# A recommender kernel on one core: all table rows fetched by GpSimd's indirect DMAs, in place of a split over five engines

## The chip, the cores and the metric

The kernel runs on one core of a Trainium2 chip. A core has five engines that matter here: TensorE (PE in the profile, with its weight loads as PEld), VectorE (DVE), ScalarE (ACT), GpSimd (POOL) and SyncE (SP). Each takes its own list of instructions in order and waits on semaphores that other engines, or landing DMAs, raise. The metric is the device time of one execution in microseconds; three runs of the kernel before took 49978.42, 49955.76 and 49929.08 us, median 49955.76.

## The reference

There are 50001 items. Every item has two embeddings of 32 numbers (`E_in`, `E_out`) and 32 neighbours. First, for each item and each of the two tables, the item attends to its neighbours:

```python
def _neighbor_attn(E, near_full):
    V = E[near_full]                       # 50001 x 32 neighbours x 32
    scores = jnp.einsum('nd,nkd->nk', E, V) / jnp.sqrt(jnp.float32(GEO_HALF))
    w = jax.nn.softmax(scores, axis=-1)
    return jnp.einsum('nk,nkd->nd', w, V)

a_sus = _neighbor_attn(E_in, near_full)
a_inf = _neighbor_attn(E_out, near_full)
h = jnp.concatenate([E_hist[history], a_sus[history], a_inf[history]], axis=-1)
t = jnp.concatenate([E_tgt[target], a_inf[target], a_sus[target]], axis=-1)
x = h * t[:, None, :]                      # 16384 users x 100 x 128
z = jax.nn.relu(jnp.einsum('bld,hd->blh', x, W1) + b1)
scores = jnp.einsum('blh,h->bl', z, W2[0])
```

Then each of 16384 users has a history of 100 items and one target item. The rows of the history are multiplied with the target's row, go through a small two-layer network, and the exponentials of the scores, masked and normalised, weight the history's rows. The total over all users and all features, one number, then enters a cosine with each target's row, and a sigmoid gives the 16384 outputs. All of it is float32.

## The kernel before

The two embeddings of an item lie side by side in `egeo`, one row of 64 numbers (256 bytes) for each item, padded to 23 x 17 x 128 = 50048 rows. The kernel has two stages.

**Stage 1** builds two tables of 128 numbers per item in DRAM, `table` (for histories) and `ttab` (for targets). It works on 391 subtiles `s` of 128 items, 17 to an iteration. An iteration's neighbour numbers `nidx` come with one DMA (`load`). For a subtile, tile `v` holds 32 neighbours' rows for each of 128 items. One indirect DMA of GpSimd (line 256) fetches one neighbour for all 128 items: 128 rows of 256 bytes, at addresses that it takes from a column of `nidx`. Tile `v` has three buffers (`n_v`, `bufs=3`). Then VectorE multiplies `v` with the item's own row (`products`, line 336), sums to scores (`scores`, 346), takes the largest (`largest`, 354 and 355); ScalarE makes the exponentials (`exponents`, 363); VectorE weights `v` (`weighted`, 377, twice), sums (`attend`, 388 and 390) and divides (`attended`, 402). A software pipeline spreads this over the steps `s`, `s+1`, `s+2` and `s+3`. Its second `weighted` is the last reader of a buffer of `v`; gathers for subtile `s+3` wait for it. The order of PE, ACT, DVE and SP in stage 1 is the program's (`manual_schedule`).

From the seventh subtile on (`NFIRST = 6`), GpSimd does not fetch all 32 neighbours. The table `egeo` is also held in SBUF, transposed (two items to a column, each number as three bfloat16 parts that add up to the float32; `transposed`, lines 184 to 202). The last six neighbours are copied out of it column by column, one instruction for one row of the 128 items: by TensorE as a multiplication with an identity (line 273), or by ScalarE or VectorE as a 6-byte copy (line 277). Each takes its address from a register; `registers` (line 204) loads 16 or 32 of these at a time. `AUX` and `COLUMN` say which engine takes which neighbour. `turn` (line 300) transposes the columns back on TensorE and adds the three parts, and `even` and `odd_half` (320, 326) copy the right half of a pair into `v`. In four of seven subtiles (`BY_ROW`) one more neighbour is fetched by SP, as 128 single DMAs of one row each (line 244), with addresses from registers. So GpSimd issues 9982 gathers in stage 1, 25.5 for a subtile on average.

**Stage 2** follows an all-engine barrier (line 516). Users stand 128 to a chunk `c` (128 chunks), and a chunk's 100 history items go in 12 groups of eight and one of four. One indirect DMA of GpSimd (line 632) fetches one history item for 128 users from `table`: 128 rows of 512 bytes. Tile `h` of a group of eight has six buffers (`u_h`). TensorE transposes the eight (647), VectorE multiplies by the target (649) and sums `h` (652), TensorE and ScalarE do the first layer (667, 668), TensorE the second (676). One gather more for each chunk fetches the targets' rows (561). SP fetches two groups of eight out of every 42 such pairs (`UNIT = 42`) row by row (`one_by_one`, line 615: 2048 single DMAs), issued two units ahead, into tile `hs` with two buffers.

Of the kernel before, what the change touches and what calls it, by code (L numbers as in the profile page):

```python
# [12 lines left out]
BF16 = mybir.dt.bfloat16  # L13
# [7 lines left out]
P = 128  # L21
# [22 lines left out]
AUX = ("PPPPPPPP", "PPPPPPPP", "AAAAAAAA", "AAAAAADD", "DDDDDDDD")  # L44
NAUX = 1 + len(AUX)
COLUMN = "PDAPP"
BY_ROW = "S.S.S.S"
NFIRST = 6
ENGINE = {"A": E.Activation, "D": E.DVE, "P": E.PE}
RUN = {"A": 16, "D": 16, "P": 32}  # L50
NREG = 32
PAIRS = ROWS // 2
NST = 3
PL = 3
GROUPS = (0, 6, 12, NSUB)

# [3 lines left out]
NG = L // LG  # L62

UG = 2
UNIT = 42
AHEAD = 4
# [3 lines left out]
def kernel(  # L70
# [18 lines left out]
    ident = nc.alloc_sbuf_tensor("ident", (P, P), F32).ap()  # L89
    ones = nc.alloc_sbuf_tensor("ones", (P, P), F32).ap()  # L90
    w1T = nc.alloc_sbuf_tensor("w1T", (D, HID), F32).ap()
    ident_b = nc.alloc_sbuf_tensor("ident_b", (P, P), BF16).ap()
    small = nc.alloc_sbuf_tensor("small", (P, 8), F32).ap()
    b1_sb = small[:, 0:1]
    w2_sb = small[:, 1:2]
# [6 lines left out]

    geo_held = nc.sbuf_tensor("geo", (P, PAIRS, PL), BF16)
    geo = geo_held.__enter__().ap()
    geo_at = nc.sbuf_base - 2 * PL * PAIRS
    geo_b = geo.rearrange("d c t -> d (c t)").bitcast(U8)

    make_identity(nc, ident)
    nc.vector.tensor_copy(ident_b, ident)
    nc.vector.memset(ones, 1.0)  # L110
    nc.sync.dma_start(b1_sb, b1.rearrange("(h o) -> h o", o=1))
    nc.sync.dma_start(w2_sb, w2.rearrange("o h -> h o"))
    with (
        tc.tile_pool(name="wsb", bufs=1) as wsb,
        tc.tile_pool(name="wps", bufs=1, space=bass.MemoryType.PSUM) as wps,
    ):
        w1_sb = wsb.tile([HID, D], F32, name="w1_sb")
        nc.sync.dma_start(w1_sb, w1)
        w1_ps = wps.tile([D, HID], F32, name="w1_ps")
        nc.tensor.transpose(w1_ps, w1_sb, ident)  # L120
        nc.vector.tensor_copy(w1T, w1_ps)
# [4 lines left out]
    egeo_v = egeo.rearrange("(i p j) d -> i p j d", p=P, j=NSUB)  # L126
    table_v = table.rearrange("(i p j) d -> i p j d", p=P, j=NSUB)
    egeo_p = egeo.rearrange("(c t) d -> c (t d)", t=2)
# [4 lines left out]
    nc.scalar.dma_start(table[:, 0:DE], ehist)  # L133
    with (
        tc.manual_schedule(engines={E.PE, E.Activation, E.DVE, E.SP}),
        tc.tile_pool(name="n_st", bufs=2) as n_st,
        tc.tile_pool(name="n_in", bufs=2) as n_in,
        tc.tile_pool(name="n_v", bufs=3) as n_v,
        tc.tile_pool(name="n_p", bufs=1) as n_p,
        tc.tile_pool(name="n_g", bufs=2) as n_g,  # L140
        tc.tile_pool(name="n_s", bufs=3) as n_s,
        tc.tile_pool(name="n_ps", bufs=1, space=bass.MemoryType.PSUM) as n_ps,
        tc.tile_pool(name="n_pb", bufs=1, space=bass.MemoryType.PSUM) as n_pb,
        tc.tile_pool(name="n_pt", bufs=2, space=bass.MemoryType.PSUM) as n_pt,
        tc.tile_pool(name="n_pc", bufs=2, space=bass.MemoryType.PSUM) as n_pc,
    ):
        egeo_b = egeo.bitcast(U8).rearrange("(o r) d -> o (r d)", o=1)
        its = {}
        subs = {}
        owns = {}  # L150

        def load(it):
            nidx = n_in.tile([P, NSUB, K], I32, name="nidx")
            nc.sync.dma_start(nidx, near_v[it])

            colf = n_p.tile([P, NSUB, NAUX + 1], F32, name="colf")
            coli = n_p.tile([P, NSUB, NAUX], I32, name="coli")
            aux = nidx[:, :, K - NAUX : K]  # L160
            nc.vector.tensor_scalar(coli, aux, 1, None, ALU.logical_shift_right)
            nc.vector.tensor_copy(colf[:, :, 1 : NAUX + 1], coli)
            nc.vector.tensor_scalar(
                colf[:, :, 1 : NAUX + 1],
                colf[:, :, 1 : NAUX + 1],
                float(2 * PL),
                float(geo_at),
                ALU.mult,
                ALU.add,
            )  # L170
            nc.vector.tensor_copy(colf[:, :, 0:1], nidx[:, :, K - NAUX - 1 : K - NAUX])
            nc.vector.tensor_scalar(
                colf[:, :, 0:1], colf[:, :, 0:1], float(8 * G), None, ALU.mult
            )
            odd = n_in.tile([P, NSUB, NAUX], I32, name="odd")
            nc.vector.tensor_scalar(odd, aux, 1, None, ALU.bitwise_and)
            n = NSUB * (NAUX + 1)
            col_ps = n_pt.tile([P, NST, P], F32, name="pt")
            nc.tensor.transpose(col_ps[0:n, 0, :], colf.rearrange("p j a -> p (j a)"), ident)
            cols = n_in.tile([n, P], I32, name="cols")  # L180
            nc.vector.tensor_copy(cols, col_ps[0:n, 0, :])
            its[it] = (nidx, odd, cols)

        def transposed(q):

            h = min(P, (PAIRS - q * NST * P))
            n = NST if h == P else 1
            st = n_st.tile([P, NST, 4 * G], F32, name="st")
            base = q * NST * P
            nc.sync.dma_start(  # L190
                st[0:h, 0:n, :],
                egeo_p[base : base + h * n, :].rearrange("(p n) d -> p n d", n=n),
            )
            into = geo[:, base : base + h * n, :].rearrange("d (p n) t -> d n p t", n=n)
            ps = n_pt.tile([P, NST, P], F32, name="pt")
            for r in range(n):
                nc.tensor.transpose(ps[:, r, 0:h], st[0:h, r, :], ident[0:h, 0:h])
            rest = ps[:, 0:n, 0:h]
            for t in range(PL):
                nc.scalar.copy(into[:, :, :, t], rest)  # L200
                if t < PL - 1:
                    nc.vector.tensor_tensor(rest, rest, into[:, :, :, t], ALU.subtract)

        def registers(s, a, engine, i0, n, low, top):
            it, j = divmod(s, NSUB)
            r = j * (NAUX + 1) + a
            _, vals = nc.values_load_multi_w_load_instructions(
                its[it][2][r : r + 1, i0 : i0 + n],
                engines=[engine],
                min_val=low,  # L210
                max_val=top,
                skip_runtime_bounds_check_because="worked out from an item's number",
            )
            return vals

        def fourth(s):
            return COLUMN[s % len(COLUMN)]

        def by_row(s):
            return s >= NFIRST and BY_ROW[s % len(BY_ROW)] == "S"  # L220

        def own_rows(s):
            if s < NT:
                it, j = divmod(s, NSUB)
                owns[s] = n_s.tile([P, 2 * G], F32, name="own")
                nc.sync.dma_start(owns[s], egeo_v[it][:, j, :])

        def gather(s):
            it, j = divmod(s, NSUB)
            nidx = its[it][0]  # L230
            v = n_v.tile([P, K, 2, G], F32, name="v")
            subs[s].update(v=v)
            if s >= NFIRST:
                for a in range(NAUX):
                    if (AUX[a - 1][0] if a else fourth(s)) in "AD":
                        subs[s]["g"][a] = n_g.tile([P, P, PL], BF16, name=f"g{a}")
            own_rows(s + 1)
            if by_row(s):
                one = n_s.tile([P, 2 * G], F32, name="one")
                subs[s]["one"] = one  # L240
                for i0 in range(0, P, NREG):
                    vals = registers(s, 0, E.SP, i0, NREG, 0, (ITEMS - 1) * 8 * G)
                    for i in range(NREG):
                        nc.sync.dma_start(
                            one[i0 + i : i0 + i + 1, :].bitcast(U8),
                            egeo_b[:, ds(vals[i], 8 * G)],
                        )
            ks = list(range(K))
            if s >= NFIRST:
                ks = ks[0 : K - NAUX + 1]  # L250
                if fourth(s) != ".":
                    ks.remove(K - NAUX)
                if by_row(s):
                    ks.remove(K - NAUX - 1)
            for k in ks:
                nc.gpsimd.indirect_dma_start(  # L256
                    out=v[:, k].rearrange("p t d -> p (t d)"),
                    out_offset=None,
                    in_=egeo,
                    in_offset=bass.IndirectOffsetOnAxis(ap=nidx[:, j, k : k + 1], axis=0),  # L260
                )

        def columns(s, a, i0):

# [28 lines left out]
        def turn(s):  # L293
            if s < NFIRST:
                return
# [506 lines left out]
```

## Time and profile before

The profiled execution took 49978.42 us, with a span of 49976.7 us from its first to its last instruction. It is one of the three runs; it lies 22.7 us (0.05%) above their median.

| what | value |
|---|---|
| span; profiled execution's time | 49976.7 us; 49978.42 us |
| stage 1, first to last gather | 8.6 to 24943.3 us |
| stage 2, first to last gather | 25000.8 to 49939.5 us |
| gathers of stage 1 (line 256) | 9982 |
| gathers of stage 2 (lines 632 and 561) | 12512 + 128 |
| SP's single-row DMAs (lines 244; 615) | 28160; 36864 |
| column copies on PE; ACT; DVE | 128128; 96096; 71456 |

How to read it: a group's line gives the source line, engine, operation, tiles written and read, count, then busy time and mean length of one instruction, and the time that the engine sat idle just before such an instruction, with what ended that idle time. "issue" means that the engine waited for nothing that the profile shows. A line of the timeline gives the start and the length in us, and, in brackets, the idle time before it and what ended that.

### The profile page before, as it was taken

To read this page: it belongs to the slowest core of one execution; us is meant where nothing else is said; L and a number is where in the kernel's file an instruction comes from. 1 tells how busy PE (TensorE), PEld (TensorE's weight loads), DVE (VectorE), ACT (ScalarE), POOL (GpSimd) and SP (SyncE) were. 2 spreads that over 40 slices of the span, in tenths; PEclk is the share of its full clock that TensorE was granted. 3 is DMA by queue.
4 is the path that set the end of the run, shared out by engine and by line. 5 is a ranking of instruction groups with operands and counts; after the bars stand their busy time and mean duration, and the time that the engine had idled before them with its cause. 6 is when DMAs were issued, how large, how long until landed. Compare 5 with 4: busy or idle time off the path is not lost. (4 is left out here: it accounts for less than half of the span.)

```text
span 49976.7 us, 727656 instructions
## 1 busy us (share of the span) xinstructions
PE 16337.4 (33%) x180208; PEld 12247.4 (25%) x180208; DVE 14789.9 (30%) x80038; ACT 14133.7 (28%) x103967; POOL 21346.3 (43%) x22628
## 2 busy tenths in 40 slices
PE   1222222222222222222244444444444444444444
PEld 1111111111111111111133222322222332222222
DVE  3444444444444444444411111111111111111111
ACT  5444444444444444444400000000000000000000
POOL 3333333333333333333355444444444554444444
PEclk9999999999999999999966666666666666666666
DMA  2000000000000000000011111111111111111111
GB/s 46 17 17 17 16 16 17 17 17 17 17 17 17 17 17 17 17 16 17 16 41 36 34 34 34 34 34 34 34 33 34 38 38 35 34 34 34 34 34 33
DMA packets 1135038, 1319.89 MB, mean 26 GB/s; under 512 B 716160, under 2 KB 765888, under 8 KB 1130784
## 3 DMA queue, kind: packets, MB, share of 16 engines
q0 software_dynamic: 723904, 1156.91, 10.3%
q1 hardware_dynamic: 204288, 65.09, 0.5%
q10 hardware_dynamic: 202592, 51.31, 0.5%
q8 instruction: 1431, 23.45, 0.2%
q14 instruction: 2823, 23.13, 0.2%
HBM read 1245.88 MB, written 51.30 MB: 26 GB/s over the span
## 5 line engine op out<-in xcount | busy, mean ns | idle before, releaser
L256 POOL DMA_INDIRECT v<-in_egeo_dram,nidx x9982 | 9421.0, 944 | 15521.9 <-issue 9728.5
L632 POOL DMA_INDIRECT h<-table,hidx x12512 | 11803.9, 943 | 8706.1 <-issue 6686.9
L277 ACT COPY g<-geo 128x6 uint8 x96096 | 10608.3, 194 | 10352.0 <-issue 8540.7
L273 PE MATMUL pc<-geo,ident_b 128*128 x128128 | 4645.3, 167 | 13959.0 <-issue 12611.7
L277 DVE COPY g<-geo 128x6 uint8 x71456 | 6458.9, 175 | 7294.4 <-issue 7284.9
L668 ACT ACTIVATE z<-z_ps,small 128x512 f32<-128x512 f32 x3200 | 2187.4, 687 | 20371.5 <-PE z_ps L667 10631.0
L273 PEld LDWEIGHTS <-ident_b 128*128 128x128 bf16 x128128 | 4096.4, 105 | 14603.2 <-issue 14601.0
L649 DVE TENSOR_TENSOR xT<-hT_ps,tT 128x1024 f32<-128x1024 f32 (+1 forms) x1664 | 1967.6, 1182 | 18197.1 <-PE hT_ps L647 9437.8
L667 PE MATMUL z_ps<-xT,w1T 128*128 128x512 f32 x6400 | 5046.6, 889 | 3861.5 <-DVE xT L649 2915.8
L676 PE MATMUL score<-small,z 128*128 128x1 f32 x25600 | 4190.6, 285 | 5506.8 <-ACT z L668 3409.4
L676 PEld LDWEIGHTS score<-small,z 128*128 128x128 f32 x25600 | 4254.0, 251 | 5914.5 <-ACT z L668 3614.9
L647 PE MATMUL hT_ps<-ident,h 128*128 128x128 f32 x12512 | 3087.4, 348 | 338.3 <-issue 240.7
L647 PEld LDWEIGHTS hT_ps<-ident,h 128*128 128x128 f32 x12512 | 2360.1, 206 | 2613.2 <-issue 2363.7
L667 PEld LDWEIGHTS z_ps<-xT,w1T 128*128 128x128 f32 x6400 | 1441.8, 275 | 4473.0 <-DVE xT L649 3147.9
L300 PE MATMUL back<-ident_b,g 128*128 128x128 bf16 x6930 | 806.1, 309 | 4829.0 <-ACT g L277 2867.8
L561 POOL DMA_INDIRECT t<-ttab,tidx x128 | 120.7, 943 | 4365.4 <-ACT z L668 4275.4
L326 DVE COPY_PREDICATED v<-odd,back 128x384 f32<-128x384 int32 x385 | 225.2, 585 | 5820.5 <-ACT v L320 5819.6
L652 DVE TENSOR_REDUCE hsum<-h 128x8 f32<-128x1024 f32 (+1 forms) x1628 | 1898.5, 1166 | 0.0
L300 PEld LDWEIGHTS <-g 128*128 128x128 bf16 x6930 | 707.6, 144 | 4843.0 <-ACT g L277 2874.1
L647 PE MATMUL hT_ps<-ident,hs 128*128 128x128 f32 x288 | 89.9, 427 | 4405.4 <-DMA hs<-table 4404.7
L377 DVE TENSOR_TENSOR big<-v,ex 128x1024 f32<-128x1024 f32 x782 | 1471.1, 1882 | 0.0
L647 PEld LDWEIGHTS hT_ps<-ident,hs 128*128 128x128 f32 x288 | 53.6, 187 | 4467.4 <-issue 4442.0
(77 smaller groups left out, 5379.9 us busy)
## 6 DMA issues: line engine op xcount, KB each, us to landing
hs<-table SPq DMA_DIRECT2D x36864, 0.5 KB
one<-in_egeo_dram SPq DMA_DIRECT2D x28160, 0.2 KB
h<-table,hidx POOLq DMA_INDIRECT x12512
v<-in_egeo_dram,nidx POOLq DMA_INDIRECT x9982
own<-in_egeo_dram SPq DMA_DIRECT2D x391, 32.0 KB
table<-in_ehist_dram ACTq DMA_DIRECT2D x1, 12512.0 KB
ttab<-in_etgt_dram ACTq DMA_DIRECT2D x1, 12500.0 KB
st<-in_egeo_dram SPq DMA_DIRECT2D x65, 192.0 KB
```

The source lines that it names most:

```text
L256: nc.gpsimd.indirect_dma_start(out=v[:, k].rearrange("p t d -> p (t d)"), out_offset=None, in_=egeo, in_offset=bass.IndirectOffsetOnAxis(a ...
L273: nc.tensor.matmul(g[:, i0 + i, :], ident_b, column, start=True, stop=True)
L277: copy(g[:, i0 + i, :].bitcast(U8), column)
L300: nc.tensor.matmul(back[:, a, :], subs[s]["g"][a][:, :, t], ident_b, start=t == 0, stop=t == PL - 1,)
L377: nc.vector.tensor_tensor(subs[s]["wv"][:, t].rearrange("p d k -> p k d"), subs[s]["v"][:, :, t, :], subs[s]["ex"][0][:, t, :] .rearrange( ...
L632: nc.gpsimd.indirect_dma_start(out=h[:, q, :], out_offset=None, in_=table, in_offset=bass.IndirectOffsetOnAxis(ap=u["hidx"][:, l : l + 1], ...
L647: nc.tensor.transpose(hT_ps[:, q, :], h[:, q, :], ident)
L649: x = nc.vector.tensor_tensor(xT[:, 0:w, :], hT_ps[:, 0:w, :], u["tT"].to_broadcast([D, w, P]), ALU.mult)
L652: s = nc.vector.tensor_reduce(u["hsum"][:, g * LW : g * LW + w], h[:, 0:w, :], AX.X, ALU.add)
L667: nc.tensor.matmul(z_ps, w1T, xT[:, q : q + LG, :], start=True, stop=True)
L668: nc.scalar.activation(z[:, q : q + LG, :], z_ps, AF.Relu, bias=b1_sb)
L676: nc.tensor.matmul(u["score"][:, l : l + 1], z[:, q, :], w2_sb, start=True, stop=True)
```

## The change

GpSimd fetches all 32 neighbours of every subtile in stage 1, and all history rows in stage 2. The table in SBUF goes, with its transposition, the column copies of PE, ACT and DVE, their register loads, the transposition back and the choice of the halves. SP fetches no rows in either stage. What is freed in SBUF goes to five buffers of `v` in place of three. An iteration's own rows now come with one DMA for 17 subtiles, and so do the `E_hist` rows of `table`, which pass through SBUF (`row`) in place of one DRAM-to-DRAM copy; `table` and `ttab` are written once in an iteration in place of three times. The order of VectorE's work in a step is now: both `weighted`, `attend`, `attended` of `s-2`, then `products`, `scores`, `largest` of `s-1`. `products` and `weighted` have a buffer each instead of one in common; PSUM tiles `own_ps` and `ex` have two. The barrier between the stages goes. Stage 2's computation stays; its groups are now all alike.

```diff
-AUX = ("PPPPPPPP", "PPPPPPPP", "AAAAAAAA", "AAAAAADD", "DDDDDDDD")
-NAUX = 1 + len(AUX)
-COLUMN = "PDAPP"
-BY_ROW = "S.S.S.S"
-NFIRST = 6
...
-UG = 2
-UNIT = 42
...
-    nc.scalar.dma_start(table[:, 0:DE], ehist)
...
-        tc.tile_pool(name="n_v", bufs=3) as n_v,
+        tc.tile_pool(name="n_v", bufs=5) as n_v,
         tc.tile_pool(name="n_p", bufs=1) as n_p,
...
             nidx = n_in.tile([P, NSUB, K], I32, name="nidx")
             nc.sync.dma_start(nidx, near_v[it])
...
+            own = n_in.tile([P, NSUB, 2 * G], F32, name="own")
+            nc.sync.dma_start(own, egeo_v[it])
+
+            row = n_in.tile([P, NSUB, D + G], F32, name="row")
+            nc.sync.dma_start(row[:, :, 0:DE], ehist_v[it])
...
-            if by_row(s):
-                one = n_s.tile([P, 2 * G], F32, name="one")
...
-            ks = list(range(K))
-            if s >= NFIRST:
-                ks = ks[0 : K - NAUX + 1]
...
-            for k in ks:
+            for k in range(K):
                 nc.gpsimd.indirect_dma_start(
...
-        def columns(s, a, i0):
...
-        def turn(s):
...
+            if j == NSUB - 1 or (it == NITER - 1 and j == NSUB - 2):
+                j0 = NSUB - 1 if it == NITER - 1 and j == NSUB - 1 else 0
                 js = slice(j0, j + 1)
...
+                nc.scalar.dma_start(ttab_v[it][:, js, DE:D], row[:, js, DE + G : D + G])
+                nc.scalar.dma_start(table_v[it][:, js, :], row[:, js, 0:D])
...
             if two:
                 weighted(s - 2, 0)
...
                 weighted(s - 2, 1)
+                attend(s - 2)
+                attended(s - 2)
             if one:
+                even(s - 1)
+                products(s - 1)
+                scores(s - 1)
+                largest(s - 1)
                 exponents(s - 1)
...
-    geo_held.__exit__(None, None, None)
-    tc.strict_bb_all_engine_barrier()
...
-        def one_by_one(c, g):
...
         def gather(c, g):
             u = users[c]
-            if (c, g) in early:
-                u["h", g] = early.pop((c, g))
-                u["got", g] = []
-                return
             h = u_h.tile([P, LW, D], F32, name="h")
```

## The prediction

> **What bounds the kernel now.** I read the page's groups first, for counts and idle time; then GpSimd's timeline beside VectorE's and ScalarE's; then the waits; and last a table by windows.
>
> ```profile
> L256 POOL DMA_INDIRECT v<-in_egeo_dram,nidx x9982 | 9421.0, 944 | 15521.9 <-issue 9728.5
> L632 POOL DMA_INDIRECT h<-table,hidx x12512 | 11803.9, 943 | 8706.1 <-issue 6686.9
> ...
> L277 ACT COPY g<-geo 128x6 uint8 x96096 | 10608.3, 194 | 10352.0 <-issue 8540.7
> ```
>
> GpSimd's queue holds nothing but gathers, and it sits idle for 15.5 of stage 1's 25 ms. The next lines say what a gather costs and what the idle time is. GpSimd in stage 1:
>
> ```profile
> 10021.12 0.94 POOL L256 DMA_INDIRECT v<-in_egeo_dram,nidx  x1 [0.30 <-issue]
> 10022.36 0.94 POOL L256 DMA_INDIRECT v<-in_egeo_dram,nidx  x1 [0.30 <-issue]
> 10057.07 0.94 POOL L256 DMA_INDIRECT v<-in_egeo_dram,nidx  x1 [33.76 <-issue]
> ...
> 10087.02 0.94 POOL L256 DMA_INDIRECT v<-in_egeo_dram,nidx  x1 [0.30 <-issue]
> 10126.67 0.94 POOL L256 DMA_INDIRECT v<-in_egeo_dram,nidx  x1 [38.70 <-issue]
> ```
>
> Back to back, gathers start every 1.249 us (0.944 busy, 0.305 between). Once a subtile GpSimd stops for some 35 us: (10126.67 - 10057.07) = 69.6 us here, on average (24943 - 568)/385 = 63.3 from the seventh subtile on, for 25.5 gathers that need 31.9. What it waits for is a buffer of `v`: the second `weighted` of the subtile three back starts at 10054.42 and takes 1.88, and the gathers go on 0.8 us later. VectorE and ScalarE, beside it:
>
> ```profile
> 10010.23 0.20 ACT L277 COPY g<-geo 128x6 uint8 x1 [1.21 <-issue]
> 10010.23 0.17 DVE L277 COPY g<-geo 128x6 uint8 x1 [1.23 <-issue]
> ...
> 10044.52 9.92 ACT L277 COPY g<-geo 128x6 uint8 x96
> ...
> 10054.42 1.88 DVE L377 TENSOR_TENSOR big<-v,ex 128x1024 f32<-128x1024 f32 x1
> ```
>
> While GpSimd gathers (until 10022), a column copy comes every 1.4 us on either engine; while it stands still (10044), 96 take 9.92 us, 0.10 each. So in stage 1 the column work bounds: it hardly moves during the gathers, holds `v` until it is done, and then the gathers wait. GpSimd and the other three work in turns.
>
> Stage 2, the waits:
>
> ```profile
> POOL t L561 <- ACT z L668: 4275.4, 17, 266.3
> ...
> PE hT_ps L647 <- DMA hs<-table: 4404.7, 20, 263.4
> ```
>
> 17 times GpSimd stands for 250 us, because TensorE waits for SP's single rows. Between those stops, and after SP's last row (it lands by 49690):
>
> ```profile
> 322.00:361.00 39.00, 5.41 (x18) 3.01 (x18) 11.59 (x14) 29.05 (x20) 29.42 (x32) 1.00 0.24 53
> 41500.00:42500.00 1000.00, 507.07 (x2161) 347.68 (x2160) 191.47 (x213) 109.43 (x176) 584.77 (x620) 0.65 0.17 42
> 49737.00:49940.00 203.00, 111.48 (x486) 80.13 (x486) 40.94 (x41) 23.96 (x36) 120.35 (x128) 0.63 0.16 42
> ```
>
> (Busy time and count of PE, PEld, DVE, ACT, POOL; then clock, DMA share, GB/s.) The last two rows are stage 2 with SP's rows and without: 1000/620 = 1.613 and 203/128 = 1.586 us for a gather, not 1.249. The reason is in the timeline: after some 20 gathers in a row TensorE's instructions come 0.7 to 1.4 us apart, the six buffers of `h` run out, GpSimd stops for 7 to 9 us. The first row is stage 1 before any column is fetched: 32 gathers in 39 us while ScalarE is busy for 29 and VectorE for 12 with a few long instructions. There nothing is slowed.
>
> **The change, part by part.**
>
> *Stage 1's gathers.* 391 x 32 = 12,512 (2530 more) at 1.249 us, if GpSimd never waits: 15,627 us. Does it wait? Each buffer of `v` is freed by a VectorE chain whose terms are rows of the kernel before: products 2.29, scores 2.28, largest 0.21 + 0.17, weighted 2 x 1.88, reciprocal 0.16, attend 2.26, attended 0.23: 11.4 us for a subtile. ScalarE has 0.21 + 2 x (0.29 + 0.19) + 0.20 = 1.4. A subtile's gathers take 40.0, so all of it lies beside them, and with five buffers the chain may be some 100 us late before GpSimd stops. The unknown is the slowing. At full starvation (1.4 us for an instruction, as in the row at 10010), nine VectorE and six ScalarE instructions add 15 x 1.4 = 21 us: 34 in all, still under 40. The lower bound is 0 added, as in the window at 322. I take 0, because after is nearest to that window: full-rate gathers, and about 15 other instructions in 40 us (70 in that window, over 1000 in the subtiles with columns).
>
> *What goes.* 128,128 column products, 167,552 copies, their register loads, transposing back, choosing halves, filling the table in SBUF during the first six subtiles (568 us for 192 gathers, which at 1.249 need 240): nothing of it is on GpSimd, so its worth is that the turns end; it is not to be subtracted again.
>
> *SP.* 28,160 and 36,864 single-row DMAs go; and so do 391 loads of 32 KB; 46 loads of 544 KB come, in SP's queue alone, half an iteration (some 340 us) ahead of their use. They are hidden by those gathers; uncovered, one would cost about as the first `nidx` load does now (8 us), 23 x 8 = 184 us at the most. ScalarE's queue: 24 x 2 table writes in place of 70 x 2; each holds nothing but ScalarE, which has 38 us to spare in a subtile. The 12.5 MB copy into `table` goes; the first gather still starts near 8.6 us.
>
> *Between the stages.* Now 57.4 us from the last gather of stage 1 to the first of stage 2. Without the barrier the first `h` must still wait for the last write of `table`; the last subtile's chain (11.4 + 1.4), two DMAs and hops remain. 20 to 60; I take 57.
>
> *Stage 2.* 12,800 + 128 gathers, 288 more than now. The 17 stops for SP's rows go (4275 us). Rate: between 1.249 (no wait at all) and 1.613; I take 1.60, between the two measured rows, as the queue to the end is the same: 12,928 x 1.60 = 20,685. What is late next is what already stops GpSimd there, the six buffers of `h`.
>
> *Sum.* 9 + 15,627 + 57 + 20,685 + 37 (last gather to the end, as now: 49976.7 - 49939.5) = 36,415 of span; the execution's time lies 2 us above its span now, so 36,417, and the median 23 us under that execution: about 36,400 us, 27% under 49,956.
>
> [...] Gathers start 1.249 us apart here, 66 in a row at the start of stage 2, so none waits for the one before. [...]
>
> **The rivals.**
>
> (a) *Stage 1 gets stage 2's stops.* Its gathers, too, cost 1.60 us each: 25,440 x 1.60 + 103 = 40,800. For it: the other engines are slowed within 10 us of the gathers' start at 10057. Against: those streams are dense in short instructions, and the window at 322 shows none of it.
>
> (b) *Stage 2 loses its stops.* SP's rows slowed TensorE, and without them gathers run at 1.249: 25,440 x 1.249 + 103 = 31,900. Against: 1.586 after SP's end.
>
> (c) *Slower than before: hand-overs between engines take as long as at the start of stage 2.* There, in 66 gathers without a stop:
>
> ```profile
> 25080.15 0.69 ACT L668 ACTIVATE z<-z_ps,small 128x512 f32<-128x512 f32 x1 [57.73 <-remote]
> ```
>
> TensorE's product for it had ended at 25047, 31 to 33 us earlier, with nothing else in its way. A subtile has two such hand-overs in its loop (VectorE's scores to ScalarE, exponents back). At 31 us each, 11.4 + 1.4 + 62 = 75 us for a subtile, 29,300 in stage 1, 50,100 in all. It decides above (49,950 - 20,788)/391 = 74.6 us for a subtile. Against: this stretch had TensorE's queue full and SP issuing; the five buffers also stop GpSimd, and when it stops, hand-overs become short.
>
> (d) *The change does not do what it says*: the order of GpSimd's queue in the changed kernel holds 12,512 gathers of `v`, then 12,800 of `h` and 128 of `t`; excluded.
>
> **How the numbers follow.** Less than 0.2% is about what a measurement of this kernel can't tell from no change. My forecast 0.74, with a range of its own from 35,900 (stage 2 at 1.56) to 37,400 (stage 1 at 42 us for a subtile, stage 2 at 1.61); (a) 0.12; (b) 0.07; (c) 0.04; something between (a) and (c) 0.03, of which a third ends within 0.2%. The range from 35,000 (stage 2 at 1.49) to 41,000 holds the forecast and (a), 0.86. Faster 0.95, within 0.01, slower 0.04.
>
> **What would show it.** Right: in stage 1 GpSimd's idle time is 0.30 before nearly every gather, its busy share 0.944/1.249 = 76%, the first gather of stage 2 near 15,690 us; no wait of TensorE for SP; in stage 2 stops of 7 to 9 us, 1.6 us a gather. Wrong: waits of line 134 for `weighted` (rival a, or c if they are long), a busy share of 76% in stage 2 too (b), gathers longer than 0.944, or starts more than 1.25 us apart without a wait.

## The result, and the profile after

The changed kernel takes 37,770.2 us (median of four runs, 37,742.74 to 37,820.4) against 49,967.09 us (four runs): a ratio of 0.756, 95% interval 0.7548 to 0.7574. The forecast was 36,400 us, 1,370 us too low.

| part (gathers: first to last) | forecast, us | profiled execution, us | difference |
|---|---|---|---|
| lead-in to the first gather | 9 | 9.3 | 0 |
| stage 1, 12,512 gathers | 15,627 (1.249 each) | 17,489 (1.398 each) | +1,862 |
| between the stages | 57 | 18.4 | -39 |
| stage 2, 12,928 gathers | 20,685 (1.600 each) | 20,226 (1.565 each) | -459 |
| last gather to the end | 37 | 42.5 | +5 |
| span | 36,415 | 37,785.6 | +1,371 |

One term carries the miss: stage 1's time for a gather. The groups of the changed kernel that answer to GpSimd's two groups before:

```profile
L331 POOL DMA_INDIRECT h<-table,hidx x12800 | 12103.0, 946 | 7964.2 <-issue 6303.3
L134 POOL DMA_INDIRECT v<-in_egeo_dram,nidx x12512 | 13335.2, 1066 | 4163.2 <-issue 4073.6
```

Stage 1's gathers (line 134) now last 1066 ns on average, not 944, and the idle time in front of them is 4163/12,512 = 0.33 us each. GpSimd's waits say that it is never stopped there:

```profile
POOL h L331 <- issue: 6303.3, 12252, 21.4
POOL v L134 <- issue: 4073.6, 12243, 1.1
POOL h L331 <- PE hT_ps L346: 1325.3, 232, 11.5
```

The longest idle time before a gather of `v` is 1.1 us, and no line says `weighted`; the 35-us stops have gone. No line names `t` waiting for ScalarE either (4275 us before): SP's stops have gone too. What is left in stage 2 are stops before `h`. So the time is lost almost wholly inside the gathers (0.12 of 0.15 us each; the idle time before them grew by 0.03). GpSimd's timeline in stage 1, at the beginning and later:

```profile
100.72 0.95 POOL L134 DMA_INDIRECT v<-in_egeo_dram,nidx  x1 [0.30 <-issue]
101.97 0.94 POOL L134 DMA_INDIRECT v<-in_egeo_dram,nidx  x1 [0.30 <-issue]
103.22 0.94 POOL L134 DMA_INDIRECT v<-in_egeo_dram,nidx  x1 [0.30 <-issue]
...
5007.45 0.99 POOL L134 DMA_INDIRECT v<-in_egeo_dram,nidx  x1 [0.30 <-issue]
5009.30 1.94 POOL L134 DMA_INDIRECT v<-in_egeo_dram,nidx  x1 [0.86 <-issue]
5011.54 1.10 POOL L134 DMA_INDIRECT v<-in_egeo_dram,nidx  x1 [0.30 <-issue]
5012.94 1.10 POOL L134 DMA_INDIRECT v<-in_egeo_dram,nidx  x1 [0.30 <-issue]
5014.34 1.09 POOL L134 DMA_INDIRECT v<-in_egeo_dram,nidx  x1 [0.30 <-issue]
```

At 100 us a gather starts every 1.25 us, as forecast. Later some start 1.40 us apart, a few 2 us, the rest 1.25. The table by windows shows that the mean is the same everywhere once it has set in (busy time and count of PE, PEld, DVE, ACT, POOL; granted TensorE clock, DMA share, GB/s):

```profile
9.00:249.00 240.00, 0.00 (x0) 0.00 (x0) 55.98 (x47) 6.51 (x30) 181.49 (x192) 1.00 0.39 84
3000.00:4400.00 1400.00, 0.00 (x0) 0.00 (x0) 344.31 (x279) 32.64 (x186) 1067.06 (x1002) 1.00 0.15 28
20000.00:21400.00 1400.00, 726.00 (x3105) 490.51 (x3103) 273.18 (x302) 157.46 (x257) 843.64 (x893) 0.65 0.17 43
```

240/192 = 1.25 us in the first 240 us; then 1002 gathers in 1400 us, 1.40. From the eighth subtile on, each subtile takes 44.8 us = 32 x 1.400 on average. In stage 2 (last row) 893 fit into the same time, 1.57. Within a burst they start 1.25 us apart; 541 times the distance is over 4 us, 8.4 us on average. One such stop:

```profile
22033.40 2.07 PE L366 MATMUL z_ps<-xT,w1T 128*128 128x512 f32 x2 [4.33 <-issue]
...
22046.75 0.94 POOL L331 DMA_INDIRECT h<-table,hidx  x1 [0.30 <-issue]
22048.98 0.69 ACT L367 ACTIVATE z<-z_ps,b_sb 128x512 f32<-128x512 f32 x1 [21.90 <-remote]
...
22055.03 0.94 POOL L331 DMA_INDIRECT h<-table,hidx  x1 [7.33 <-PE hT_ps L346]
```

TensorE's product for the first half of a group ends at 22035.5; ScalarE, idle for 21.90 us, takes it up at 22048.98, 13.5 us later and only after GpSimd has stopped. "remote" marks such a wait: no instruction of the profile ended just before it was over. The transposes that free the buffer of `h` come later still, at 22051.45 and 22054.22.

### The profile page after: what moved, and what is told of

The parts are those of the page before. It is cut to its first block, busy times and chain, and to the rows that moved or that the text cites. A ratio compares the mean times of both kernels' runs of the same rounds, so it can differ in the third digit from the quotient of the medians.

```text
span 37785.6 us, 138256 instructions
## 1 busy us (share of the span) xinstructions
PE 10340.1 (27%) x44931; PEld 7001.1 (19%) x44931; DVE 8310.6 (22%) x7885; ACT 2701.7 (7%) x6067; POOL 25560.0 (68%) x25446
## 3 DMA queue, kind: packets, MB, share of 16 engines
q0 software_dynamic: 814080, 1258.87, 15.0%
## 4 chain that ended last, share of the span: by engine, by line
POOL 34%; another core or an unknown queue 28%; PE 17%; issue 16%; DVE 3%; ACT 2%; DMA 0%; POOLq 0%; ACTq 0%; DVEq 0%; SPq 0%
POOL v L134 34%; PE z_ps L366 9%; PE score L375 5%; PE hT_ps L346 3%; DVE xT L348 2%; ACT z L367 1%; DVE hsum L351 1%; DVE wv L190 0%; DVE prod L150 0%; DVE att L203 0%; DVE sc L160 0%; ACT ea L381 0%; ACT junk L311 0%; PE hT_ps L305 0%
## 5 line engine op out<-in xcount | busy, mean ns | idle before, releaser
L331 POOL DMA_INDIRECT h<-table,hidx x12800 | 12103.0, 946 | 7964.2 <-issue 6303.3
L134 POOL DMA_INDIRECT v<-in_egeo_dram,nidx x12512 | 13335.2, 1066 | 4163.2 <-issue 4073.6
L375 PE MATMUL score<-w_sb,z 128*128 128x1 f32 x25600 | 3958.2, 276 | 3932.1 <-ACT z L367 3124.4
L375 PEld LDWEIGHTS score<-w_sb,z 128*128 128x128 f32 x25600 | 3960.4, 239 | 4188.3 <-ACT z L367 3336.0
L150 DVE TENSOR_TENSOR prod<-v,own_ps 128x2048 f32<-128x2048 f32 x391 | 894.3, 2287 | 12689.2 <-DMA v<-in_egeo_dram,nidx 12688.9
L367 ACT ACTIVATE z<-z_ps,b_sb 128x512 f32<-128x512 f32 x3200 | 2192.1, 687 | 15457.2 <-PE z_ps L366 6899.3
L190 DVE TENSOR_TENSOR wv<-v,ex 128x1024 f32<-128x1024 f32 x782 | 1407.6, 1876 | 362.3 <-ACT ex L177 257.6
L177 ACT ACTIVATE ex<-sc,top 128x32 f32<-128x32 f32 x782 | 227.7, 291 | 16990.5 <-DVE top L168 9583.0
L160 DVE TENSOR_REDUCE sc<-prod 128x64 f32<-128x2048 f32 x391 | 894.5, 2288 | 13.5
L203 DVE TENSOR_REDUCE att<-wv 128x64 f32<-128x2048 f32 x391 | 893.7, 2286 | 12.7
```

The source lines that it names most:

```text
L134: nc.gpsimd.indirect_dma_start(out=v[:, k].rearrange("p t d -> p (t d)"), out_offset=None, in_=egeo, in_offset=bass.IndirectOffsetOnAxis(a ...
L150: nc.vector.tensor_tensor(prod.rearrange("p k t d -> p k (t d)"), v.rearrange("p k t d -> p k (t d)"), subs[s]["own"].to_broadcast([P, K, ...
L160: nc.vector.tensor_reduce(sc.rearrange("p t k -> p k t"), subs[s]["prod"], AX.X, ALU.add)
L190: nc.vector.tensor_tensor(subs[s]["wv"][:, t].rearrange("p d k -> p k d"), subs[s]["v"][:, :, t, :], subs[s]["ex"][0][:, t, :] .rearrange( ...
L203: nc.vector.tensor_reduce(att, subs[s]["wv"], AX.X, ALU.add)
L331: nc.gpsimd.indirect_dma_start(out=h[:, q, :], out_offset=None, in_=table, in_offset=bass.IndirectOffsetOnAxis(ap=u["hidx"][:, l : l + 1], ...
```

## The experiments

Three theories stood for the 1.40 us of stage 1: VectorE's and ScalarE's work beside the gathers lengthens them (A); GpSimd can't keep up more than one gather in 1.40 us, whatever the others do (B); the reuse of a buffer of `v` does it, through the waits it puts into GpSimd's queue (C). The kernel before, run beside the first eleven experiments, took 50,498 to 50,555 us, 1.1% more than in the result, so what is compared is the stage times of each trace. Each of these eleven is one execution. Stage 2, in runs that leave it as it is, took 20,226, 20,282, 20,360 and 20,500 us: differences under about 1.5% there say nothing.

**1. Little VectorE work in stage 1**

```diff
+        def short(s):
+            it, j = divmod(s, NSUB)
+            nc.vector.tensor_copy(
+                its[it][2][:, j, DE:D], subs[s]["v"][:, K - 1].rearrange("p t d -> p (t d)")
+            )
...
-            if two:
-                weighted(s - 2, 0)
...
             if one:
...
-                products(s - 1)
...
+                short(s - 1)
```

> The changed kernel with stage 1's attention left out: for each subtile VectorE copies one neighbour's 64 numbers into `row` (128x64), and products, scores, exponents, weighted and attend are not computed, so the table's right halves are not the reference's. Gathers, buffers of v and stage 2 stay. Stage 1 now takes 17,490 us, 1.398 us from gather to gather, where 1.249 was forecast. Theory A (VectorE's and ScalarE's 13 us of work per subtile lengthen the gathers beside them): stage 1 falls to 12,512 x 1.249 = 15,630 us, the total to 35,900. Theory B (gathers cannot be kept up faster than 1.40 us, whatever the others do; 1.249 holds only for the first 200): 17,490 stays, total 37,750. Theory C (the lengthening follows the reuse of a buffer of v, through the waits that it puts into GpSimd's queue): 17,490 stays too. Stage 2 20,230 under all.

Stage 1 took 17,487 us, total 38,041.72.

**2. VectorE's long operations twice** (`summed` is the sum over `wv`, taken out of `attend`)

```diff
+                for _ in range(2):
                     weighted(s - 2, 0)
                     weighted(s - 2, 1)
+                    summed(s - 2)
...
+                for _ in range(2):
                     products(s - 1)
                     scores(s - 1)
```

> The changed kernel with VectorE's long operations of stage 1 done twice (products, scores, both weighted, the sum of attend): 22 us of VectorE's work per subtile in place of 11.4, still under the 40 to 45 us of a subtile's gathers; the result is unchanged. Theory A: the excess over 1.249 us, 4.8 us per subtile, doubles: 49.6 us per subtile, stage 1 19,380 us, total 39,650. Theory B and theory C: stage 1 stays at 17,490, total 37,770.

Stage 1: 17,484 us, total 37,842.88. The same window of the first run:

```profile
3000.00:4400.00 1400.00, 0.00 (x0) 0.00 (x0) 6.10 (x31) 6.75 (x31) 1092.21 (x1000) 1.00 0.14 28
```

and of the second:

```profile
3000.00:4400.00 1400.00, 0.00 (x0) 0.00 (x0) 673.46 (x438) 32.65 (x186) 1083.53 (x1001) 1.00 0.14 28
```

VectorE is busy for 6 us or for 673 us, and 1000 or 1001 gathers fit. Theory A falls. What VectorE does decides only which gathers of a subtile are the long ones: with little work 9,616 of them start about 1.40 us apart, with double work 7,227 at about 1.25 and 1,347 at 2.0 to 2.2; the sum is the same.

**3. Twelve buffers of `v`** (`bufs=5` to `bufs=12`)

> The changed kernel with twelve buffers of v in place of five. In the changed kernel the first six subtiles are gathered at 1.249 us, the seventh and all later ones at 1.40. Theory A: VectorE works in the second subtile already, so nothing new; 17,490. Theory B with a backlog that fills in some 200 gathers: 1.40 from the seventh subtile on as now; 17,490. Theory C: 1.249 until the buffers are first used again, so for 12 or 13 subtiles, then 1.40: 17,460 us.

Stage 1: 17,488 us, total 37,920.99. The first subtile above 40.2 us is the seventh, the eighth takes 44.8, long before a buffer is used a second time. Theory C falls; B holds.

**4. Twenty-four buffers of `h` in stage 2** (`bufs=6` to `bufs=24`)

> The changed kernel with 24 buffers of h in stage 2 in place of 6. Stage 2 now takes 20,226 us: 1.25 us per gather inside the bursts and 652 stops of some 8 us. If the stops come only because six buffers are too few to ride over a late stretch of TensorE and ScalarE: the stops go, stage 2 is 12,928 x 1.25 = 16,160 us and the total 33,700. If the other engines are held back for as long as GpSimd gathers, so that the stops only become rarer and longer: stage 2 stays within 2% of 20,226. If a ceiling of 1.40 us per gather applies here as in theory B: 18,100, total 35,640.

Stage 2 took 21,741 us, worse by 1,500, total 39,388.14. GpSimd's waits name the next buffer in line:

```profile
POOL t L293 <- ACT z L367: 3203.0, 124, 28.4
POOL h L331 <- PE hT_ps L346: 142.8, 115, 25.5
```

By the distances from gather to gather there are 379 over 4 us, 15.9 us on average, in place of 541 of 8.4. Of these, 125 of 26.8 us stand before `t`, which has two buffers, once for nearly every chunk; 254 of 10.5 us are left before `h`, about two for each chunk, most of them put down to "issue" and so not in the line with 142.8. More room made the stops fewer and longer and didn't end them.

**5. What does the ceiling count? Gathers of 64 rows; and stage 2 without computation**

```diff
-                    out=v[:, k].rearrange("p t d -> p (t d)"),
+                    out=v[0 : P // 2, k].rearrange("p t d -> p (t d)"),
...
-                    in_offset=bass.IndirectOffsetOnAxis(ap=nidx[:, j, k : k + 1], axis=0),
+                    in_offset=bass.IndirectOffsetOnAxis(ap=nidx[0 : P // 2, j, k : k + 1], axis=0),
...
-                nc.tensor.transpose(hT_ps[:, q, :], h[:, q, :], ident)
...
+            nc.vector.tensor_copy(u["hsum"][:, g * LW : g * LW + w], h[:, 0:w, 0])
```

> Two stages, two questions; both leave out the computation, so the outputs are not the reference's. Stage 1: attention left out as in the first run, and each gather fetches 64 rows (partitions 0 to 63) in place of 128. If the ceiling of 1.40 us counts rows, it falls to 0.70 us and GpSimd's own time bounds: at most 1.249 us for a gather, stage 1 at most 15,640. If it counts gathers: 17,490. Stage 2: transposes, products, both layers left out; VectorE copies 8 numbers of each group of h, so that GpSimd hardly ever waits for a buffer. If the ceiling holds here too and does not count bytes (512-byte rows in place of 256): 12,928 x 1.40 = 18,100 us. If there is no ceiling in stage 2 and all of its loss is waiting for TensorE: 12,928 x 1.25 = 16,150. If the ceiling counts bytes: over 20,226.

Total 35,625.28 us; windows of stage 1 and stage 2:

```profile
3000.00:4400.00 1400.00, 0.00 (x0) 0.00 (x0) 9.13 (x62) 6.75 (x31) 1074.70 (x1001) 1.00 0.09 16
...
20000.00:21400.00 1400.00, 4.47 (x10) 1.82 (x10) 41.17 (x209) 9.63 (x40) 1047.79 (x1000) 1.00 0.18 47
```

Stage 1 took 17,483 us with half the rows, though the first 150 gathers now came 1.21 us apart. Stage 2 took 18,098 us for 12,927 steps: 1.400, with rows of 512 bytes. Both stages have the same ceiling, and it counts neither rows nor bytes.

**6. Half the bytes in stage 1; three buffers of `h`** (source `egeo.rearrange("r (t d) -> (r t) d", t=2)`, `out=v[:, k, 0]`; `u_h` `bufs=3`)

> Stage 1: attention left out as in the first run, and each gather fetches 128 rows of 128 bytes in place of 256 (so the table is not the reference's). If the ceiling counts bytes: GpSimd's own 1.249 us bounds, stage 1 15,640. If it counts rows or gathers: 17,490. Stage 2: three buffers of h in place of 6, computation whole. 24 buffers gave 1.682 us per gather against 1.565 with six, with stops fewer and longer. If the engines work in turns, and short turns are better: under 1.565, stage 2 19,000 to 20,100. If six was already the best, and three leave GpSimd waiting for each group's chain: 1.6 to 1.8, 20,700 to 23,300.

Stage 1: 17,487 us. Stage 2: 20,512. Total 38,043.97. Bytes are out; three buffers are as good as six within what one execution can tell, so turns made shorter by fewer buffers gain nothing.

**7. One part of the change alone: the kernel before without SP's rows in stage 2** (`units = []`)

> The kernel before with one part of the change alone: SP fetches no rows in stage 2, so GpSimd fetches all 12,800 + 128; stage 1 and its columns stay. The forecast's own step: the 17 stops (4,275 us) go, and 288 gathers more come, 12,928 x 1.565 to 1.60 = 20,230 to 20,690 us in place of 24,939: 4,250 to 4,700 us off the total. If SP's rows also slow the others between the stops (rival b): more, down to 12,928 x 1.25 = 16,150, 8,800 off. If the stops have another cause: less than 1,000 off.

Total 45,523.74 us beside 50,512.21. Stage 2 took 20,316 us in place of 24,939, 1.572 for a gather. By the stages this part is worth about 4,600 us, as forecast; by the two totals, one execution each, 4,990 us, some 300 above the range given. The rest, 24,935 to 17,489 = 7,446 us, is stage 1, where the columns, SP's rows and the order of VectorE's work changed together; no run parts these. Rival (b) falls: without SP's rows the stops of 4 to 12 us stay (542, 8.6 us on average).

**8. Three buffers of `v`, four of `h`**

> The changed kernel with the three buffers of v that the kernel before had, in place of five; and with four buffers of h in place of six. Stage 1: if what freed the gathers is the column work alone, three buffers do as well: the last weighted of a subtile is over some 13 us after the next subtile's gathers have landed, 30 us before the buffer is wanted again; 17,490 us. If five are needed: GpSimd stops at each subtile, some 13 us or more, 22,600 us. Stage 2, four buffers: between the values for three and six; under 20,226 if shorter turns are better.

Stage 1: 17,487 us; stage 2: 20,416; total 37,968.47. Three, five and twelve buffers of `v` give the same stage 1: the two more buffers that the change bought with the freed SBUF are worth nothing.

**9 and 10. Gathers of stage 2 paced by a memset**

```diff
+    pad = const.tile([P, 128], F32, name="pad")
...
+                nc.gpsimd.memset(pad, 0.0)
```

The memset stands behind each `indirect_dma_start` of `h`; the second run has 384 columns in place of 128.

> The changed kernel with one GpSimd memset of a 128x128 tile after each gather of stage 2 (0.21 us for that shape at the kernel's start), so that gathers start some 1.40 to 1.50 us apart instead of 1.249. Theory D (gathers issued faster than 1.40 us build up a backlog of some 200 x 0.15 = 30 us, and while it lasts the other engines' hand-overs are late; so paced gathers leave them alone): the stops of 4 to 12 us go, stage 2 takes 12,928 x 1.45 = 18,750 us (18,100 to 19,400), total 36,300. Theory E (the other engines are slowed whenever GpSimd gathers, whatever its pace): the stops stay and the memsets come on top, stage 2 20,300 to 23,000.

> As the run before, with a memset of 128x384: some 0.2 us longer, gathers 1.60 to 1.70 us apart. Theory D: no stops at all, 12,928 x 1.65 = 21,300 us (20,700 to 22,000), nearly all of it GpSimd's own pace. Theory E: the stops stay, 22,000 us and more.

With 128 columns the gathers came 1.334 us apart (part of the memset's 0.22 us fits into the idle time before a gather, which falls from 0.30 to 0.17), below the ceiling; stage 2 took 19,926 us, with 471 stops over 4 us, now 6.7 on average; total 37,523.64. With 384 columns they came 1.548 apart, above it: one stop over 4 us, stage 2 20,016 us, total 37,573.30. The waits that tell the two apart are VectorE's for something that no instruction of the profile ended. In the changed kernel, then with 128, then with 384 columns:

```profile
DVE xT L348 <- remote: 6284.5, 466, 41.9
```

```profile
DVE xT L350 <- remote: 10185.6, 837, 60.7
```

```profile
DVE xT L350 <- remote: 73.3, 2, 56.6
```

The late hand-overs go when the gathers are slower than the ceiling, and not when they are slowed a little less. That agrees with theory D as far as the pace goes; theory E, that the others are slowed at any pace, falls. The granted TensorE clock isn't behind it: from 26,000 to 35,000 us it was 0.65 in the changed kernel, 0.61 with 128 columns and 0.55, the lowest, with 384. The gain alone is small: stage 2 is 1.5% and 1.0% shorter than the changed kernel's 20,226 us, about what single executions differ by. Neither time lies in the range worked out for theory D, because the memsets space the gathers less than was assumed, 1.334 and 1.548 us in place of 1.45 and 1.65: so the first run stayed under the ceiling and kept its stops, and the second ended earlier.

**11. Fewer TensorE instructions in the second layer**

```diff
-                nc.tensor.matmul(
-                    u["score"][:, l : l + 1], z[:, q, :], w2_sb, start=True, stop=True
-                )
+                nc.tensor.matmul(
+                    u["sT"], w2_at[:, n, :], z[:, q : q + LG, :], start=n == 0, stop=n == NG - 1
+                )
...
+            nc.scalar.copy(sT, u["sT"])
...
+                nc.tensor.transpose(score[:, q, :], sT[:, q, :], ident[0:NG, 0:NG])
```

> The changed kernel with the second layer done by fewer TensorE instructions: in place of 100 products with one output column for each chunk, 25 products with w2 in one of 25 columns, summed into one PSUM tile of 25 rows by 512, then one copy and four transposes: 155 TensorE instructions for a chunk in place of 226, the same result. If the stops of stage 2 come from TensorE's instructions being spaced out while GpSimd gathers: the excess over the ceiling, 0.165 us per gather, shrinks by a third to a half, stage 2 18,900 to 19,500, total 36,400 to 37,000. If they come from late hand-overs between engines, of which there are as many as before for a group: 20,226 within 2%. If the ceiling is all that is left: 18,100.

Stage 2: 19,115 us (1.479), inside the first theory's range; total 36,677.93. 379 stops, 8.9 us on average. The order of TensorE's instructions changed as well, so their number alone isn't shown to be the cause; and the granted TensorE clock was higher here (0.71 from 26,000 to 35,000 us, 0.65 in the changed kernel).

**12. Both: paced just above the ceiling, and fewer TensorE instructions** (`pad` of 232 columns)

> Both edits that gained: the second layer with 155 TensorE instructions for a chunk, and a memset after each gather of stage 2, of 128x232 (from 1.334 us per gather with 128 columns and 1.547 with 384, 1.42 is worked out, just above the ceiling of 1.400). Theory D: no backlog, so hardly a stop over 4 us; stage 2 12,928 x 1.42 = 18,360 us (18,250 to 18,700), stage 1 17,490 as before, total 35,900; 35,616 is 25,440 gathers at 1.400. If the other engines still fall behind at this pace: stops stay and stage 2 is 18,900 to 19,400, total 36,500 to 37,000, no better than fewer TensorE instructions alone.

Five runs: median 36,026.58 us (36,026.53 to 36,026.9), ratio to the kernel before 0.7213, 95% interval 0.7203 to 0.7223; the changed kernel stands at 0.7561 against the same kernel. GpSimd in stage 2, and its waits:

```profile
25001.18 0.95 POOL L336 DMA_INDIRECT h<-table,hidx  x1 [0.17 <-issue]
25002.13 0.31 POOL L343 MEMSET pad<- 128x232 f32 x1
25002.61 0.95 POOL L336 DMA_INDIRECT h<-table,hidx  x1 [0.16 <-issue]
```

```profile
POOL h L336 <- issue: 2135.6, 12611, 3.4
POOL h L336 <- PE hT_ps L352: 48.0, 92, 6.5
```

A gather every 1.425 us, two stops over 4 us, stage 2 18,463 us. GpSimd does more work and the kernel is 1,740 us faster than the changed one: stage 2 fell by 1,110 us with fewer TensorE instructions, and by 650 more (3.4%) when the gathers were paced too. All 25,440 gathers at 1.400 would be 35,616; 410 us are left above that.

## Why the prediction was right and wrong

- **Direction and mechanism: right.** GpSimd and the others worked in turns, and the turns ended; SP's stops went. The time lies in the range given (35,000 to 41,000), but 370 us above the end of the likeliest case's own (37,400; its terms, 42 us for a subtile and 1.61 us, add up to 37,320).
- **Stage 1's gathers: the step that failed.** "12,512 at 1.249 us, if GpSimd never waits": it never waits, and that half is right, but the price is 1.400 us once some 200 gathers have gone (runs 1 to 3, 5, 6 and 8: 17,483 to 17,488 us). The row was read from the first subtiles of the kernel before, and from runs of at most 66 gathers. That trace has no 100 gathers in a row faster than 1.48 us each, so GpSimd's own rows couldn't show what a gather costs when thousands follow each other; the range should have taken 1.249 as a lower bound there. But the figure stood in another engine's rows, in the very "1.4 us" that the prediction read as starvation. ScalarE's column copies in the kernel before, around the end of the burst of 26 gathers that runs from 9991.16 to 10022.36:

```profile
10022.13 0.20 ACT L277 COPY g<-geo 128x6 uint8 x1 [1.20 <-issue]
...
10026.33 0.20 ACT L277 COPY g<-geo 128x6 uint8 x1 [1.20 <-issue]
...
10027.73 0.68 ACT L277 COPY g<-geo 128x6 uint8 x6 [0.49 <-issue]
```

They come 1.40 us apart, not 1.25, and go on so for 4 us after the last gather. A queue that took 26 gathers from 9991.16 on, one each 1.400 us, would be empty at 10027.6, when the copies come close together again. It is so in the whole of stage 1 from 1000 us on: of 4,424 distances of 1.35 to 1.45 us between these copies, 4,421 begin while such a queue would still hold gathers (only 4,043 if it took one each 1.249 us), and the last slow copy of a burst begins 4.5 us after GpSimd's last gather in the median, where that queue would be empty after 5.05. So the trace before had the sustained price in it. It also agrees with theory D: dense short instructions of other engines are slow (here 1.40 us apart, then six in 0.68 us) until the gathers are worked off at 1.400 us each.
- **"I take 0" for the slowing of VectorE's and ScalarE's chain by the gathers: right.** In the window at 3000, VectorE's work is 344.31 us for 31.25 subtiles, 11.0 for a subtile where 11.4 was summed. The 4.8 us that a subtile took longer are in GpSimd's gathers themselves, for which the sum had no such term.
- **Five buffers: not needed.** The forecast counted on them for cover; three are as good (run 8).
- **Columns, SP, loads, table writes: right** to be costed at nothing beyond the end of the turns. The waits after name them only at the first load (8.0 us, GpSimd) and at the last table write (3.4 us before an `h`).
- **Stage 2: mechanism right, rate 2% high** (1.565 for 1.60). Taking the rate of the last 203 us was a short sample of what run 7 gives as 1.572 over all of stage 2. **Between the stages:** 18.4 us, below the range's lower end of 20; 57 was too high.
- **Rival (a)**, stops in stage 1: none came. **Rival (b)**: stops stayed without SP (run 7). **Rival (c)**, hand-overs of 31 us in stage 1: none came; ScalarE's first exponential started 0.03 us after VectorE's maximum (5005.40 after 5005.37). In stage 2 late hand-overs are real, as run 10 shows by removing them.
- **"None waits for the one before": right for the landing, not for the price.** From a gather's start to the end of its last packet it is 2.2 us in the median, and the next gather of stage 1 starts 1.40 us after it on average, before that end. The price of one gather after another is 1.400 us all the same, for rows of 128, 256 and 512 bytes alike (runs 6, 3 and 5), not 1.249.

What stays open is why it is 1.400. The profile counts 32 packets for each gather (814,080 for the 25,440): 16 of 4 bytes, and 16 with the rows, of 2,048 bytes in stage 1 and 4,096 in stage 2. Whether the price follows their number is not shown. The packets don't pile up: taken in order of time, a gather's last 4-byte packet has ended 2.2 us after the gather's start in the median and 3.1 us in all but 1%, though GpSimd's lead over a pace of 1.400 is 23 us or more in stage 1 once it has built up. VectorE starts on a subtile 3.4 us after the start of its last gather, too. So what is worked off at 1.400 us isn't seen in the DMA packets, nor in how soon the gathers' landing is known in stage 1. Nor is it shown why stage 1's hand-overs stay short (0.03 us from `largest` to the first exponential) while GpSimd is held at 1.40.

## What to carry to other kernels

Take the price of an instruction that will fill a queue for milliseconds from a stretch that is as long and as dense; a price from a short burst was a lower bound here (1.249 for 1.400 us). Look at the other engines' rows as well: a regular distance between their instructions during the burst can be the sustained price (1.40 us between column copies here). Where a saturated queue delays other engines' hand-overs, try pacing it to just above its sustained rate: here that ended nearly all late hand-overs (73 us of such waits of VectorE at a gather every 1.548 us, in place of 6,285), while 24 buffers of `h` in place of six left 379 stops. What it gains depends on what else bounds the stage (within the noise by itself, 3.4% of stage 2 once TensorE had fewer instructions). Ask also whether the stage that gets all the work has a floor: 25,440 gathers of 1.40 us are 35,616 us, and no run here that kept their number got below that.

## What was not expected of the hardware

- GpSimd's indirect DMAs in a row: 1.25 us each (1.21 with 64 rows) for the first 185 to 225, then 1.400 on average, in all twelve traces that gather 12,512 times in stage 1, with 128 or 64 rows, 256 or 128 bytes, three to twelve buffers. GpSimd's lead over a pace of 1.400 grows to 30 to 35 us at first and then stays between 23 and 35. The late hand-overs at the start of stage 2 before (31 to 33 us) have about that size; that the two are one thing is not shown.
- The lead comes back in the next bursts: after a stop, gathers run at 1.25 us again, while ScalarE's and VectorE's column copies beside them (kernel before) come 1.400 us apart.
- Pacing gathers at 1.334, 1.425 and 1.548 us left 471, 2 and 1 stops over 4 us: the change lies between the first two, where 1.400 is. (The run at 1.425 also had fewer TensorE instructions, which alone left 379.)
